# A two-layer Perceiver kernel: the planner that orders its instructions gets measured lengths, overlaps and an exclusion of VectorE and GpSimd, and the context gets one buffer per batch

## The chip, the cores and the metric

The kernel runs on one core of one Trainium2 chip. A core has five engines that each run a queue of instructions in order: PE (TensorE, matrix multiplication), DVE (VectorE), ACT (ScalarE), POOL (GpSimd) and SP (SyncE, which here only issues DMA transfers). The metric is the device time of one execution in microseconds (us); lower is better. The profile is that of one execution on the chip.

## The reference

The input `x` holds 32 batches of 64 tokens by 256 features, `ctx` holds 32 batches of 256 context tokens by 256. Six blocks follow each other, each added to `x`:

```python
x = x + L0_xattn(ctx, layernorm(x))   # q = LN(x) Wq; k, v = [LN(ctx), LN(x)] Wkv; 16 heads of 64; softmax over 320 keys; Wo
x = x + L0_attn(layernorm(x))         # linear attention: relu(q), relu(k), kv = k^T v, q kv / (q sum k), then a layer norm
x = x + L0_ffn(layernorm(x))          # silu(x Wg) * (x Wu) Wd, int8-valued weights, hidden 768
x = x + L1_xattn(layernorm(x), ctx)   # 16 heads of 16, masked softmax over 256 keys
x = x + L1_attn(layernorm(x))         # sLSTM: gated recurrence over 64 tokens, 64 units
x = x + L1_ffn(layernorm(x))          # router with entmax over 8 experts, then each expert's 256-1024-256 MLP
```

All of it is float32. The 2048 tokens make 16 tiles of 128 tokens, two batches each.

## The kernel before, in words

*Stages.* The first cross attention (L0) runs over batches `b` (32), tiles `t` of two batches (16) and groups `g` of four batches (8). `l0_context(t)` loads the context of the two batches of a tile, normalises it (`norm`) and multiplies and adds the layer norm's weights (`affine`, two GpSimd instructions). `l0_queries(g)` makes the queries of a group, then folds the key weights into them (`pqk`, `qk`). `l0_keys(b)` transposes the context (`tr_c`). `l0_scores(b)` makes eight score tiles `sc` of 128 x 320 per batch; for each, VectorE takes the maximum (`nmax`) and ScalarE the exponential; then VectorE scales four of them at once (128 x 1280), and turns them in blocks of 32 x 32 (three `transpose`). The blocks are put into `pT` by sixteen copies of 32 x 640: four on GpSimd, four on ScalarE or VectorE, eight as SyncE transfers. `l0_applied(b)` multiplies them with the context (`pu`), `l0_projected(t)` does the value and output weights (`po`, `pw`). Layer 1 and the rest of layer 0 then run in groups of two tiles: `linear_attention` (tiles `lak`, `lakv`, `lakvs`, `lac`, `laq`, `tr_la`), `feed_forward`, `queries`, `keys_values`, `scores` (`xsc`), `weighted` (`xpTp` transposes, `xpo`), `projected`, `slstm_router` (`slg`, `slp`, `tr_me`). Last come the experts: entmax in two parts A and B (`gT_psA`, `gT_psB`), the lists of tokens, gathers with indirect DMAs, `expert` (`tr_xga`, `mepha`, `mepya` for large buckets of tokens, `tr_xgb`, `mephb`, `mepyb` for small ones), and a scatter of each expert's result that adds to `out`.

*Order.* None of this is run as it is written. The calls on `pl` only record operations, each with its rank (a due time), its engine and what it reads and writes. A few matmuls recorded inside `pl.together(length)` are one operation; `pl.either` and `pl.copy` record an operation that ScalarE or VectorE may run. `Plan.run` then simulates the five engines: again and again it takes, among the operations that could be next, the one with the earliest start by its own model (ties by rank), on the engine where it starts first, and issues it. The instructions stay in this order on each engine. Every recorded instruction is therefore issued from one line, L375 (`issue`) before and L420 after, and the profile must be read by tiles. The model's lengths are in `PlanEngine.length` (L470); an operation may not start before its engine is free and its inputs are done, with `HOP` = 0.06 between engines.

*Buffers.* `bank` takes one of eight PSUM banks. The SBUF tiles named `arena` lie in one large tensor, in areas that `ar.put(phase, tag, size, places...)` lays out; an area's places are used in turn, and a tile can be issued only when its place is free. The context's area `cx` (L652) has two places of 1024 elements, each with one tile of two batches (4 x 256 per partition).

## Time and profile before

| what | value |
|---|---|
| time, median of 3 runs | 1632.85 us (1630.63 to 1634.4) |
| the profiled execution: its time | 1633.02 us |
| its span (first to last instruction) | 1631.3 us |
| mean granted PE clock | 0.991 |
| instructions in the span | 25951 |
| moved by DMA | 95.02 MB, 58 GB/s on average |

The busy share of each engine is the sum of its instructions' durations over the span; matmuls are pipelined, so PE counts as busy while several overlap. The span has three parts of different mix: L0 cross attention up to about 850 us, the groups of layer 0 and 1 from there to about 1400, the experts after it. A row of the stage table is one stretch: its length, each engine's busy time with the instructions that started in it, the granted PE clock (1.00 is full speed), the DMA engines' busy share and GB/s. In a list of waits, a row says which tile's instruction waited for which engine and tile, the total, how often, and the longest.

### The profile page before, as it was taken

What the parts mean: (1) busy time and instruction counts of PE and PEld (TensorE: products, weight loads), DVE (VectorE), ACT (ScalarE), POOL (GpSimd) and SP (SyncE); (2) the same over time, 40 slices, a digit from 0 to 9 for tenths busy, and PEclk for the clock granted to TensorE, in tenths of its full rate; (3) what the DMA queues carried; (4) which work ended last, traced back from release to release, by engine and by line L of the source; (5) the groups of instructions that cost most, each with busy time, mean ns of one, the idle gap of its engine ahead of it and who ended that gap; (6) DMA issues with size and microseconds to landing.
All of it is one profiled execution on the core that took longest, in us unless ns stands there. A gap on an engine that the chain in (4) does not pass through costs nothing. (4 is left out here: it accounts for less than half of the span.)

```text
span 1631.3 us, 25951 instructions
## 1 busy us (share of the span) xinstructions
PE 1579.4 (97%) x9226; PEld 1106.8 (68%) x9226; DVE 1088.2 (67%) x3089; ACT 693.8 (43%) x1813; POOL 422.1 (26%) x524
## 2 busy tenths in 40 slices
PE   8999999999999999999989999999999999999996
PEld 6556656565665656666556777777777776878885
DVE  6657666676766757776755788888888788762230
ACT  4434344353533535334421454454544547432332
POOL 5123123230333223331311221221212112223342
PEclk9999999999999999999999999999999999999998
DMA  6112112121112211122121000010000220455391
GB/s 212 38 30 59 38 31 44 38 59 29 39 30 46 47 34 40 30 71 53 38 54 49 14 27 27 18 37 14 27 27 20 85 80 19 133 144 141 69 307 31
DMA packets 95601, 95.02 MB, mean 58 GB/s; under 512 B 9327, under 2 KB 85936, under 8 KB 95472
## 3 DMA queue, kind: packets, MB, share of 16 engines
q1 hardware_dynamic: 89952, 85.41, 19.2%
q0 software_dynamic: 5520, 7.94, 2.4%
q8 instruction: 74, 1.21, 0.3%
q14 instruction: 55, 0.45, 0.1%
HBM read 63.63 MB, written 7.47 MB: 44 GB/s over the span
## 5 line engine op out<-in xcount | busy, mean ns | idle before, releaser
L375 PE MATMUL pu<-arena 128*128 128x512 f32 (+1 forms) x768 | 301.0, 615 | 3.5 <-ACT arena L375 2.8
L375 PE MATMUL sc<-arena 128*128 128x320 f32 x1024 | 290.5, 436 | 0.0
L375 PEld LDWEIGHTS sc<-arena 128*128 128x128 f32 x1024 | 190.8, 190 | 95.3 <-issue 19.2
L375 ACT ACTIVATE arena<-sc,nmax 128x320 f32<-128x320 f32 x256 | 134.4, 527 | 250.3 <-DVE nmax L375 241.8
L375 PEld LDWEIGHTS pu<-arena 128*128 128x128 f32 (+1 forms) x768 | 113.9, 189 | 175.9 <-issue 159.1
L375 POOL COPY arena<-arena 32x640 f32<-32x640 f32 (+1 forms) x161 | 108.9, 676 | 404.1 <-DVE arena L375 300.4
L375 DVE TENSOR_REDUCE nmax<-sc 128x1 f32<-128x320 f32 x256 | 121.8, 484 | 105.5 <-PE sc L375 104.1
L375 POOL TENSOR_TENSOR arena<-arena 128x1024 f32<-128x1024 f32 (+3 forms) x72 | 118.5, 1646 | 166.6 <-DVE arena L375 109.7
L375 ACT ACTIVATE arena<-arena,xnm 128x256 f32<-128x256 f32 x256 | 127.1, 500 | 52.1 <-DVE xnm L375 51.9
L375 DVE COPY arena<-pu 128x512 f32<-128x512 f32 x62 | 42.7, 689 | 115.4 <-PE pu L375 115.2
L375 DVE CUSTOM_DVE_ANT_0 arena<-xsc,arena 128x256 f32<-128x256 f32 x256 | 101.2, 421 | 17.7 <-ACT arena L375 10.3
L375 DVE TENSOR_TENSOR arena<-arena,sm 128x1280 f32<-128x1280 f32 x64 | 108.1, 1690 | 2.2
L375 DVE STREAM_TRANSPOSE arena<-arena 128x512 f32<-128x512 f32 (+1 forms) x192 | 104.4, 594 | 3.6
L375 ACT COPY arena<-pu 128x512 f32<-128x512 f32 x66 | 38.4, 585 | 128.0 <-PE pu L375 128.0
L375 POOL DMA_INDIRECT out<-arena x25 | 39.6, 1585 | 102.8 <-DVE arena L375 71.2
L375 PE MATMUL pqk<-arena 64*128 64x256 f32 x512 | 63.1, 383 | 1.6 <-ACT arena L375 1.6
L375 PE MATMUL xpTp<-ident,arena 128*128 128x128 f32 x512 | 63.6, 274 | 0.9 <-ACT arena L375 0.9
L375 PE MATMUL xak<-arena 128*128 128x512 f32 x128 | 62.3, 610 | 0.0
L375 PEld LDWEIGHTS xpTp<-ident,arena 128*128 128x128 f32 x512 | 56.9, 141 | 7.2 <-DVE arena L375 2.2
L375 PE MATMUL xav<-arena 128*128 128x256 f32 x256 | 61.5, 384 | 0.0
L375 PEld LDWEIGHTS po<-arena 128*64 128x64 f32 x1024 | 55.5, 137 | 8.8 <-issue 8.3
L375 PE MATMUL mepha<-arena 128*128 128x256 f32 x256 | 60.1, 385 | 1.4 <-ACT arena L375 1.4
(395 smaller groups left out, 2800.9 us busy)
## 6 DMA issues: line engine op xcount, KB each, us to landing
arena<-in_m_w SPq DMA_DIRECT2D x26, 1024.0 KB
arena<-arena SPq DMA_DIRECT2D x256, 80.0 KB
arena<-in_ctx SPq DMA_DIRECT2D x32, 256.0 KB
arena<-in_ctxT SPq DMA_DIRECT2D x16, 512.0 KB
x<-in_x SPq DMA_DIRECT2D x16, 128.0 KB
arena<-in_l0x_wkv SPq DMA_DIRECT2D x2, 1024.0 KB
arena<-arena SPq DMA_DIRECT2D x16, 128.0 KB
out<-x SPq DMA_DIRECT2D x16, 128.0 KB
```

The source lines that it names most:

```text
L375: r = getattr(real, name)(*[get(a) for a in args], **{k: get(a) for k, a in kw.items()})
```

## The change

It has three parts.

1. `Plan.run`'s model. An engine counts as free a little before its operation ends (`OVERLAP`: DVE 0.085, ACT 0.11, POOL 0.05); an operation that needs another's result starts 0.03 after it on the same engine and `HOP` after it on another; a group of matmuls counts 0.985 of its length; and the start of an operation that takes a new place or PSUM bank is not before that place is free (`since`, `when`), which before was only added after the choice. `locks` names VectorE operations (three full-size SBUF operands, or a copy or tensor-scalar operation from SBUF to SBUF of 64 elements or more) and all GpSimd operations but memset as excluding each other: one is not planned to start while the other is held.
2. The lengths in `PlanEngine.length`.
3. The context has one tile of 2 x 256 per batch: `cx` has four places of 512, `affine` is called once per batch with width 2 (128 x 512) in place of once per tile with width 4 (128 x 1024), and `l0_keys` and `l0_applied` index the tile of their batch.

What is computed and the number of matmuls stay as they were. The diff, cut to what the text speaks of:

```diff
@@ -161,6 +162,9 @@
     def room(self, t_, k):
         return len(self.free) > k and (not self.in_order or self.asked[self.next + k] is t_)
 
+    def when(self, k):
+        return sorted(self.free)[k]
+
     def take(self, t_):
         self.free.sort()
         self.next += 1
@@ -186,6 +190,10 @@
             return False
         return all(a.next == len(a.asked) and a.live[j] is None for a, j in self.rivals[i])
 
+    def when(self, k):
+        i = (self.next + k) % len(self.places)
+        return max([self.last[i]] + [a.last[j] for a, j in self.rivals[i]])
+
     def take(self, t_):
         i = self.next % len(self.places)
         self.next += 1
@@ -219,6 +227,7 @@
 
     ENGINES = {"PE": "tensor", "DVE": "vector", "ACT": "scalar", "POOL": "gpsimd", "SP": "sync"}
     HOP = 0.06
+    OVERLAP = {"DVE": 0.085, "ACT": 0.11, "POOL": 0.05}
 
     def __init__(self, tc):
         self.tc, self.ops, self.slots, self.news = tc, [], {}, []
@@ -254,7 +263,7 @@
         self.group = []
         yield
         calls, self.group = self.group, None
-        self.add({"PE": (length, calls)})
+        self.add({"PE": (0.985 * length, calls)})
 
     def add(self, ways):
         op = Op()
@@ -300,6 +309,8 @@
         free = dict.fromkeys(self.ENGINES, 0.0)
         busy = dict.fromkeys(self.ENGINES, 0.0)
         wire = 0.0
+        hold = {"DVE": (0.0, 0.0), "POOL": (0.0, 0.0)}
+        calls_lock = self.locks
         ready = [op for op in self.ops if op.left == 0]
         todo = len(self.ops)
         waiting = set(self.ops)
@@ -318,12 +329,17 @@
                     if "PE" in op.ways and (short is None or op.rank < short.rank) and self.has_room(op, True):
                         short = op
                     continue
+                since = self.since(op)
                 for engine, (length, _) in op.ways.items():
-                    at = free[engine]
+                    at = max(free[engine], since)
                     for other in op.before:
-                        at = max(at, other.end if other.on == engine and other.end == other.done else other.done + self.HOP)
+                        at = max(at, other.done + (0.03 if other.on == engine else self.HOP))
                     for t_ in op.uses:
                         at = max(at, t_.free_at)
+                    if engine in hold:
+                        (lo, hi), other = hold[engine], calls_lock(op.ways[engine][1][0], engine)
+                        if other and lo <= at < hi:
+                            at = hi
                     key = at, op.rank
                     if best is None or key < best[0]:
                         best = key, op, engine
@@ -334,8 +350,11 @@
             ready.remove(op)
             waiting.remove(op)
             op.on = engine
-            op.end = op.done = free[engine] = at + length
+            op.end = op.done = at + length
+            free[engine] = op.end - self.OVERLAP.get(engine, 0.0)
             busy[engine] += length
+            if engine in hold and self.locks(calls[0], engine):
+                hold["POOL" if engine == "DVE" else "DVE"] = at, op.end
             if "dma" in calls[0][0]:
                 size = PlanEngine.size_of(calls[0])
                 wire = max(wire, op.end) + size / 380e3
@@ -347,6 +366,22 @@
                     ready.append(other)
         self.now, self.busy = max(op.done for op in self.ops), busy
 
+    @staticmethod
+    def locks(call, engine):
+
+        name, args, kw = call
+        if engine == "POOL":
+            return name != "memset"
+        if name not in ("tensor_tensor", "scalar_tensor_tensor", "tensor_copy", "tensor_scalar"):
+            return False
+        views = [a for a in list(args) + list(kw.values()) if isinstance(a, View)]
+        size = [math.prod(v.shape[1:]) for v in views]
+        views = [v for v, n in zip(views, size) if n == max(size)]
+        inner = [v for v in views if not isinstance(v.tile.slots, Slots) or v.tile.slots.in_order]
+        if name in ("tensor_tensor", "scalar_tensor_tensor"):
+            return len(inner) >= 3
+        return max(size) >= 64 and len(inner) == len(views)
+
     def has_room(self, op, later=False):
 
         taken = {}
@@ -359,6 +394,16 @@
                 return False
             taken[id(s_)] = k + 1
         return True
+
+    def since(self, op):
+
+        at, taken = 0.0, {}
+        for t_ in op.news:
+            k = taken.get(id(t_.slots), 0)
+            taken[id(t_.slots)] = k + 1
+            if t_ in op.uses:
+                at = max(at, t_.slots.when(k))
+        return at
 
     def issue(self, op, engine, calls):
         for t_ in op.news:
@@ -483,15 +528,17 @@
                 m *= k
             n = max(n, m)
         if name == "memset":
-            return 0.1 + 0.5e-3 * n
+            return 0.12 + 0.5e-3 * n
         if engine == "ACT":
             if isinstance(kw.get("scale"), View):
                 return 0.6
-            return (0.12 + 0.91e-3 * n if name == "copy" else 0.33 + 0.66e-3 * n) + (0.19 if "accum_out" in kw else 0)
+            return (0.12 + 0.91e-3 * n if name == "copy" else min(0.33 + 0.66e-3 * n, 0.6)) + (0.09 if "accum_out" in kw else 0)
         if engine == "DVE":
-            return 0.15 + 1.04e-3 * n + (0.08 if name == "tensor_tensor_reduce" else 0)
+            return 0.15 + 1.04e-3 * n + (0.02 if name == "tensor_tensor_reduce" else 0)
         if engine == "POOL":
-            return 0.7 if n < 64 else 0.3 + 2.0e-3 * n
+            if n < 64:
+                return 0.7 if n <= 2 else 1.0
+            return 0.15 + 0.97e-3 * n if name == "tensor_copy" else 0.3 + 1.9e-3 * n
         return 0.18 if name == "transpose" else max(0.36, 1.67e-3 * n)
 
 
@@ -649,7 +696,7 @@
         ar.put(1, "gb", 1024, 10240)
         for n, tag in enumerate(("la", "ls", "latT")):
             ar.put(1, tag, 512, 11264 + 512 * n, 12800 + 512 * n)
-        ar.put(1, "cx", 1024, 14336, 15360)
+        ar.put(1, "cx", 512, *range(14336, 16384, 512))
         ar.put(1, "cT", 640, 16384, 17024)
         ar.put(0, "gbcol", 256, 17664, 17920)
         ar.put(1, "qk", 1024, *range(17664, 25856, 1024))
@@ -774,12 +821,11 @@
         def l0_context(t):
 
             pl.rank = 2 * t - 6.0
-            cx = ar.tile([P, 4, D], F32, tag="cx", name=f"cx{t}")
+            cx = [ar.tile([P, 2, D], F32, tag="cx", name=f"cx{t}_{b2}") for b2 in range(2)]
             for b2 in range(2):
                 b = 2 * t + b2
                 pl.sync.dma_start(
-                    out=cx[:, 2 * b2 : 2 * b2 + 2, :],
-                    in_=d["ctx"][b * S2 : (b + 1) * S2, :].rearrange("(t p) d -> p t d", p=P),
+                    out=cx[b2], in_=d["ctx"][b * S2 : (b + 1) * S2, :].rearrange("(t p) d -> p t d", p=P)
                 )
             if t == 0:
                 load_w(wv, "l0x_wkv", slice(1024, 2048))
@@ -794,9 +840,10 @@
                 pl.sync.dma_start(out=nxt["rows_a"], in_=d["rows"][:, 0 : 4 * D].to_broadcast([P, 4 * D]))
                 pl.sync.dma_start(out=rows, in_=d["rows"][:, 4 * D :].to_broadcast([P, NROWS - 4 * D]))
             pl.rank = 2 * t - 3.0
-            srcs = [cx[:, i, :] for i in range(4)]
+            srcs = [cx[i // 2][:, i % 2, :] for i in range(4)]
             norm(srcs, srcs, f"c{t}", "c")
-            affine(cx, 0, 4)
+            for b2 in range(2):
+                affine(cx[b2], 0, 2)
             return cx
 
         def l0_queries(g):
@@ -861,7 +908,7 @@
             with pl.together(T4):
                 for kd in range(KD):
                     for i in range(2):
-                        tr(pst[:, kd, i * P : (i + 1) * P], cx[:, 2 * b2 + i, kd * P : (kd + 1) * P], ident)
+                        tr(pst[:, kd, i * P : (i + 1) * P], cx[b2][:, i, kd * P : (kd + 1) * P], ident)
             pl.gpsimd.tensor_copy(cT[:, :, S2:SK], lt[:, :, b4 * S : (b4 + 1) * S])
             pl.copy(cT[:, :, 0:S2], pst)
             return cT
@@ -936,7 +983,7 @@
                     with pl.together(1.75):
                         for n in range(2):
                             rhs = pT[:, 2 * n + jj].rearrange("p a j c -> p j a c")
-                            mm(pus[jj], cx[:, 2 * b2 + n, f_], rhs, start=(n == 0), stop=False)
+                            mm(pus[jj], cx[b2][:, n, f_], rhs, start=(n == 0), stop=False)
                 with pl.together(1.04):
                     for jj in range(2):
                         h_ = slice(64 * jj, 64 * jj + 64)
```

More of the change, by code (lines that the diff above doesn't have):

```diff
@@ L1 @@
+import math
 from contextlib import ExitStack, contextmanager
```

## The prediction

> **What bounds the kernel now.** I read the page's busy shares first, then busy time by stage, then the list of what the TensorE (PE) waits for, then the timeline at the longest waits.
>
> ```profile
> PE 1579.4 (97%) x9226; PEld 1106.8 (68%) x9226; DVE 1088.2 (67%) x3089; ACT 693.8 (43%) x1813; POOL 422.1 (26%) x524
> ```
>
> PE has work for 97% of the 1631.3 us, so the program is a chain of matmuls with holes in it. No other engine is near its limit over the whole. The change touches no matmul, so all that it can gain lies in the holes. Where they are (columns of the stage table: stretch in us, its length, busy time of PE, PE weight load, VectorE, ScalarE, GpSimd with instruction counts, granted clock, DMA share, GB/s):
>
> ```profile
> 0.00:20.00 20.00, 12.22 (x46) 9.70 (x47) 9.72 (x39) 7.18 (x13) 8.54 (x28) 1.00 0.91 302
> ...
> 68.00:95.00 27.00, 23.93 (x99) 13.20 (x96) 20.16 (x39) 10.62 (x28) 7.14 (x10) 0.94 0.31 69
> 95.00:790.00 695.00, 692.80 (x3351) 436.98 (x3352) 473.17 (x919) 294.26 (x715) 196.71 (x194) 1.00 0.19 41
> 790.00:850.00 60.00, 54.28 (x240) 31.82 (x238) 35.80 (x62) 20.95 (x53) 9.12 (x15) 0.98 0.19 43
> ...
> 905.00:1300.00 395.00, 389.66 (x2979) 291.47 (x2980) 318.71 (x1149) 196.69 (x571) 76.02 (x142) 1.00 0.09 29
> 1300.00:1400.00 100.00, 95.76 (x801) 71.66 (x797) 83.66 (x341) 61.74 (x185) 18.33 (x33) 1.00 0.21 67
> ...
> 1568.00:1600.00 32.00, 28.00 (x164) 24.68 (x163) 10.88 (x65) 7.21 (x23) 18.15 (x17) 0.89 0.80 243
> 1600.00:1631.30 31.30, 17.52 (x113) 15.93 (x111) 2.76 (x7) 7.35 (x22) 4.73 (x4) 0.85 0.08 10
> ```
>
> PE's idle time is length less busy. The long cross-attention stretch (95–790) leaves 2.2 us of 695; the start 7.8, the seam of the first two layers 5.7, six layer-1 groups 5.3, the end of layer 1 4.2, the end of the experts 4.0, the last 31 us 13.8 (the last matmul ends at 1617.5; a scatter and the closing follow). In all 52 us. Busy time hides a part: matmul records overlap (a 320-column record is 436 ns long, but they start every 269 ns), so each wait is 0.16–0.19 us longer than its gap. The waits:
>
> ```profile
> PE lakvs L375 <- DVE arena L375: 5.3, 1, 5.3
> PE gbp L375 <- DVE tok L610: 5.3, 1, 5.3
> PE pu L375 <- ACT arena L375: 2.8, 1, 2.8
> PE gT_psB L375 <- DVE arena L375: 2.4, 1, 2.4
> PE xpo L375 <- DVE arena L375: 2.1, 11, 0.2
> PE mephb L375 <- issue: 2.0, 2, 1.2
> PE tr_la L375 <- ACT arena L375: 1.8, 5, 0.4
> PE pqk L375 <- ACT arena L375: 1.6, 7, 0.2
> ```
>
> Five are single places, the rest recur. Some are followed by a half-speed clock:
>
> ```profile
> 79.10:82.50 3.40, 2.88 (x4) 1.37 (x5) 3.24 (x6) 0.06 (x1) 0.00 (x0) 0.50 0.00 0
> 847.10:854.00 6.90, 3.37 (x24) 2.75 (x25) 5.83 (x19) 1.44 (x2) 3.22 (x5) 0.51 0.50 95
> ```
>
> **The change part by part.** I compared both programs' instruction orders. The 9226 matmul records' worth of work is the same. VectorE goes from 3089 to 3053 instructions, ScalarE from 1300 to 1336 (queue counts without accumulator reads), GpSimd from 538 to 570.
>
> *Context in one buffer per batch.* GpSimd runs two 128x512 affine operations where it ran one of 128x1024, 32 times: 2 x 1351 − 2526 ns = +0.18 us each, +5.6 us in all. GpSimd is busy 26–28% there, so its idle time hides it; uncovered it would cost those 5.6. SyncE issues the same 448 instructions; the context loads stay in pairs at the same queue places, and only the two swaps of the latents move behind eight more pT transfers, which is one batch (about 26 us; 27 batches fill 95–790); they stay issued more than two batches ahead of the group that reads them, and that slack hides the move. Zero.
>
> *Exclusion of VectorE and GpSimd.* The row: the softmax scaling, `TENSOR_TENSOR arena<-arena,sm 128x1280`, takes 1690 ns on average (64 times), and 1491–1493 where GpSimd is quiet: 64 x 0.2 = 13 us of blocking. The Trainium skill, "SBUF — State Buffer", section "SBUF: two separate sides", calls the shared port an exclusive lock, where the second instruction blocks fully. Read as time, that rule promises up to 13 us. The row beside it says otherwise: VectorE is 68% busy in 95–790 (473 of 695) while PE lacks 2.2 us, so the 13 us lie beside matmuls. I count nothing for the lock itself, and it speaks against the change that keeping an instruction back delays it for certain to avoid a delay that wasn't on the path.
>
> *Recalibrated lengths and `since`.* These only reorder. By place:
>
> 1. Mode changes of PE. Before, each batch runs 12 `sc`, 12 `pu`, 4 `sc`; after, they interleave, yet changes between full and 64-row matmuls fall from 410 to 399. One costs about 0.2 us (523 against 429 ns at the step into 64 rows, +104 at the way out): **−2**.
> 2. `pu` of batch 1. Its wait is 2.94 us, and half clock for 3.4 us costs 1.7 more. PE's work between its last `sc` and it grows from 9.5 to 11.0 us. The Trainium skill, "TensorE: Matmul & The Clock Gate", section "HAM oscillation", warns of idle gaps over some 3.4 us; this row throttles after 2.9. By the rule the place is worth 1.5; by the row up to 3.2. I go by the row, halfway: **−2.3** (−1.5 to −3.5).
> 3. Steady cross attention. The `pqk` waits (7 x 0.60, for a bank that ScalarE's copy frees; `since` now sees this) and three at `pu` (0.37) total 5.3. Between a batch's last `sc` and its `pu` there are now 15–17 us of PE work (before 12.7–18); the chain needs about 11.3 (point 4). **−4** (0 to −6).
> 4. The seam. From the last `sc` of batch 31 (842.7) the chain is softmax, scaling, transposes to 847.5, eight transfers, `pu` at 854.0: 11.3 us.
>
> ```profile
> 842.70 1.88 PE L375 MATMUL lakv<-arena 128*128 128x512 f32 x4
> ...
> 847.20 5.16 SPq L375 DMA_DIRECT2D arena<-arena  x8
> ...
> 850.54 1.23 PE L375 MATMUL lakvs<-arena 64*128 64x129 f32 x8 [5.32 <-DVE arena L375]
> ...
> 854.03 2.38 PE L375 MATMUL pu<-arena 128*128 128x512 f32 x5
> ```
>
> After, 26 us of work stand between the second `lakv` and its `lakvs`, so that 5.5 us wait goes; but only 3.0 us (before 4.1) stand ahead of this `pu`, which then waits 8 us or more itself. Net: 1.1 us less cover, 0.4 for a VectorE operation now ahead of the transposes, and 0 to 1.7 of half clock: **+2.5** (+1 to +3.5).
> 5. Regular layer-1 groups (67.4 us each). Waits per group: `tr_la` 0.79, `xpo` 0.92, `tr_me` 0.31, `slg` 0.18, so 2.2, and 13 over six groups. Cover grows at `slp`→`tr_me` (4.1 to 5.5) and `xaq`→`xsc` (3.7 to 18.5), stays 0.6 at `xpTp`→`xpo`, and shrinks at `xsc`→`xpTp` of odd tiles (5.5 to 4.3, and 5.8 to 5.2, where about 4.1 is needed), `slg`→`slp` (5.7 to 4.7, 4.15 needed) and `tr_la`→`laq` (3.0 to 1.7). I take half: **−6** (−13 to +5).
> 6. End of layer 1, same joints, 8 us of waits: **−3** (−8 to +3).
> 7. `gT_psB` at 1450.5: 2.5 us and 1.7 of half clock. Its cover grows from 8.2 to 11 us, 10.7 are needed: **−4** (−2 to −4.2).
> 8. The experts' end. A 128x1 VectorE operation waits for a scatter, ahead of the evacuation that frees a bank for the next matmuls:
>
> ```profile
> 1584.63 0.16 DVE L375 TENSOR_TENSOR arena<-arena 128x1 int32<-128x1 f32 x1 [4.53 <-DMA out<-arena]
> 1585.32 0.42 DVE L375 TENSOR_TENSOR arena<-mepyb,arena 128x256 f32<-128x256 f32 x1 [0.53 <-PE mephb L375]
> ```
>
> From `mephb` at 1581.4 to the next `mephb` at 1595.8 are 14.5 us for 8.05 of spacing, so 6.4 are lost. After, both such evacuations stand ahead of the waiting operation, and ten of 44 gate multiplications go to ScalarE. Against it, the first evacuation is behind some 24 small VectorE operations (before 17): +1. **−5** (−2 to −6.4).
> 9. A `tr_xga` directly before its `mepha` at three places (two before): **+0.9**.
> 10. Joints that only the new order makes, which no view of the old one shows. Lower end 0, since nothing can be under no wait; upper about 8 (20 of the usual 0.4 us); nearest rows are the 0.2–0.6 us waits above: **+3**.
>
> Sum: −2 − 2.3 − 4 + 2.5 − 6 − 3 − 4 − 5 + 0.9 + 3 = −19.9. Against the profiled execution's 1633.0 (span 1631.3; 1.7 around it; 0.2 above the median of 1632.85), that gives **1613 us**. The start (7.8) and the closing (13.8) are kept.
>
> **The rivals.**
>
> A, slower: point 5 turns. Its place is layer 1, where VectorE is 81% busy (318.7 of 395). If two evacuation copies (0.59 each on ScalarE) come to stand ahead at each thinned joint, `xpTp` of odd tiles loses 1.0 x 8, `slp` 0.65 x 8, `laq` 0.6 x 16, together 23 us. Without layer 1 my sum stands at −11, so 1622 + 23 = **1645**; it decides from 11 us, half of that. For it: the shrunk covers, and more copies on ScalarE (`xpTp` 68 to 84). Against: ScalarE is half idle there.
>
> B, no real change: waits move to the next joint, as at the seam, and only the mode changes stay: **1631**. For it: 2.2 us idle in 695. Against: `gT_psB` and the tail are single places with room behind them.
>
> C, larger gain: all of 13 and 8 us in layer 1 go and point 10 is nothing: 1613 − 12 − 3 = **1598**. Against: `xpo` keeps its 0.6 cover.
>
> **How the numbers follow.** Chances: forecast 0.60 (own range 1604 to 1625), A 0.16, B 0.12, C 0.12. The measurement tells 0.2% (3.3 us) from no change. A lies above; B is half within it, half below; the rest is below: faster 0.78, same 0.06, slower 0.16. The range from 1599 to 1636 leaves out half of C and most of A.
>
> **What would show it.** Right: no PE wait near 79.6 and none at `gT_psB`; a `pu` wait of 8 us or more at the seam in place of `lakvs`; no VectorE stall of 4 us ahead of a `mepyb` evacuation; `pqk` gone from the list of waits; the 128x1280 scaling near 1.5 us with no gain of its own. Wrong: layer-1 groups longer than 67.4 us, with `xpTp`, `slp` or `laq` in the waits, or new half-clock stretches.

## The result

The changed kernel takes 1637.88 us (median of 18 runs, 1635.36 to 1641.66) where the kernel before takes 1632.56 beside it: ratio 1.0032, 95% interval 1.0022 to 1.0042. It is slower by 0.3%. I had forecast 1613 and given "slower" 0.16; the time lies above my range.

The profiled execution of the changed kernel spans 1637.4 us. Its page, and the busy time by stage (columns as in the table of before):

```profile
PE 1564.8 (96%) x9226; PEld 1099.7 (67%) x9226; DVE 1010.1 (62%) x3053; ACT 716.2 (44%) x1849; POOL 431.7 (26%) x556
```

```profile
0.00:20.00 20.00, 12.40 (x41) 9.68 (x42) 9.87 (x39) 6.59 (x12) 8.89 (x28) 1.00 0.91 303
...
68.00:95.00 27.00, 25.12 (x118) 14.00 (x118) 20.76 (x44) 12.11 (x30) 7.35 (x10) 1.00 0.31 69
95.00:790.00 695.00, 689.14 (x3352) 437.36 (x3348) 430.98 (x907) 306.24 (x728) 204.96 (x222) 1.00 0.19 41
790.00:850.00 60.00, 52.81 (x254) 32.05 (x252) 36.19 (x73) 22.03 (x54) 10.55 (x16) 0.97 0.21 47
...
905.00:1300.00 395.00, 377.58 (x2943) 282.00 (x2943) 298.28 (x1115) 197.14 (x571) 76.32 (x141) 1.00 0.09 29
1300.00:1400.00 100.00, 94.81 (x785) 71.01 (x784) 80.62 (x346) 59.76 (x177) 18.63 (x33) 0.98 0.16 51
...
1568.00:1600.00 32.00, 28.97 (x177) 26.14 (x176) 11.30 (x73) 9.07 (x28) 16.09 (x15) 0.95 0.96 302
1600.00:1637.40 37.40, 22.72 (x152) 20.35 (x150) 3.60 (x10) 8.78 (x25) 9.30 (x8) 0.88 0.13 26
```

VectorE is 78 us less busy than before (ScalarE 22 more), and yet PE is idle for longer: in the layer-1 groups (905–1300) 17.4 us where it was 5.3. Where the time went is best read between matmuls that both orders have, by the start of the first matmul of a tile in both traces (us). The last column is the same difference between a second profile of each kernel (e15 and e16 below, both from one chip):

| from the start, then from mark to mark | before | changed | difference | second pair |
|---|---|---|---|---|
| to `pu` of batch 1 | 79.62 | 80.19 | +0.6 | −0.5 |
| to `pu` of batch 30 (first cross attention) | 751.55 | 749.83 | −1.7 | −1.9 |
| to the first `ffd` of group 1 (the seam) | 101.64 | 103.60 | +2.0 | +0.1 |
| five regular groups | 337.20 | 343.10 | +5.9 | +5.9 |
| to the first `mephb` (end of layer 1, large buckets) | 269.75 | 270.64 | +0.9 | +1.3 |
| to the last `mepyb` (small buckets) | 77.39 | 75.53 | −1.9 | +1.0 |
| all, from the start to the last matmul | 1617.14 | 1622.89 | +5.8 | +5.9 |

The groups, the first cross attention and the end of layer 1 repeat; the start, the seam and the small buckets do not, so two profiles can't tell there what is the change's and what is the execution's.

The regular groups take 68.63 us in place of 67.41. What PE waits for in 905–1300, the longest rows, first before, then changed (total us, times, longest):

```profile
PE xpo L375 <- DVE arena L375: 1.9, 10, 0.2
PE tr_la L375 <- ACT arena L375: 1.8, 5, 0.4
PE xsc L375 <- DVE arena L375: 0.4, 1, 0.4
```

```profile
PE laq L420 <- DVE arena L420: 7.3, 5, 1.5
PE slp L420 <- DVE arena L420: 5.4, 5, 1.1
PE xrT L420 <- DVE r_xa L420: 2.8, 6, 0.5
PE tr_me L420 <- DVE arena L420: 0.8, 5, 0.2
```

The waits of before are all but gone, as forecast. Three others, longer ones, took their place. Per group, counted from start to start of the matmuls (so with the part that overlapping records hide), `laq` waits 1.63, `slp` 1.15, `xrT` 0.64 and a few small ones 0.2: 3.6 us, against 2.4 of before. The difference, 1.2, is the group's whole loss.

`laq` and `slp` wait for VectorE. The row of `xrT` names `r_xa`, which is VectorE's too, but in the code the `xrT` transposes read only what the GpSimd operation `arena<-xsm,arena` wrote, and it ends 0.01 to 0.02 us before `r_xa` in all six places (lines in the last section). That GpSimd operation in its turn starts 0.17 us after VectorE's reciprocal of `xsm`, which is 0.55 us behind the plan (described below), so the lateness comes from VectorE here as well, one step back.

This is how one of the waits looks, in the timeline of the changed kernel (start, duration, engine, instruction, idle time before it and what ended it; ... marks lines left out):

```profile
960.94 0.54 DVE L420 TENSOR_SCALAR arena<-xaq,pp,hm 128x256 f32<-128x256 f32 x1
961.52 0.56 ACT L420 ACTIVATE arena<-xaq,arena,hm 128x256 f32<-128x256 f32 x1 [0.46 <-DVE arena L420]
962.12 0.54 DVE L420 TENSOR_SCALAR arena<-xaq,pp,hm 128x256 f32<-128x256 f32 x1 [0.63 <-ACT arena L420]
...
962.65 0.68 DVE L420 COPY arena<-tr_la 128x512 f32<-128x512 f32 x1
...
963.39 1.35 PE L420 MATMUL laq<-arena 128*128 128x256 f32 x5 [1.47 <-DVE arena L420]
```

The copy of `tr_la` could have run from 960.2, when its transposes were done. It stood in VectorE's queue behind work that came late. I wrote out the start that the planner had given to each operation and set it beside the trace, relative to the matmuls: at 958 us VectorE is already 1.15 us behind its plan; the evacuations of `xaq` (their copies out of PSUM), which VectorE and ScalarE do by turns, waiting for each other, add 1.0 more. The plan has no wait at `laq` at all. The same list shows where the plan's cover came from (cover is the PE work that stands between an operation's producer and the matmul that needs its result): layer-1 matmul groups are planned too long (planned length, which is the number in the code times 0.985, against the median advance in the trace): `xsc` 1.43 against 1.08, `xpo` 0.79 against 0.51, `slg` 1.58 against 0.95, `lac` 0.89 against 0.62, `lakvs` 0.89 against 0.65, `slp` 0.49 against 0.31. With 4, 8, 2, 2, 2 and 2 of them in a group, the planner sees 6.3 us of matmuls per group that don't exist.

### The profile page after: what moved, and what is told of

It reads as the page before. It is cut to its first block, busy times and chain, and to the rows that moved or that the text cites. A ratio compares the mean times of both kernels' runs of the same rounds, so it can differ in the third digit from the quotient of the medians.

```text
span 1637.4 us, 25998 instructions
## 1 busy us (share of the span) xinstructions
PE 1564.8 (96%) x9226; PEld 1099.7 (67%) x9226; DVE 1010.1 (62%) x3053; ACT 716.2 (44%) x1849; POOL 431.7 (26%) x556
## 5 line engine op out<-in xcount | busy, mean ns | idle before, releaser
L420 PE MATMUL pu<-arena 128*128 128x512 f32 (+1 forms) x768 | 305.9, 616 | 6.9 <-DMA arena<-arena 5.3
L420 POOL COPY arena<-arena 32x640 f32<-32x640 f32 (+1 forms) x161 | 117.2, 728 | 430.7 <-DVE arena L420 389.6
L420 POOL TENSOR_TENSOR arena<-arena 128x512 f32<-128x512 f32 (+2 forms) x104 | 120.5, 1180 | 114.5 <-DVE arena L420 84.2
L420 DVE TENSOR_TENSOR arena<-arena,sm 128x1280 f32<-128x1280 f32 x64 | 100.7, 1573 | 1.9
L420 ACT COPY arena<-arena 32x640 f32<-32x640 f32 x115 | 83.1, 723 | 22.7 <-DVE arena L420 21.3
L420 POOL TENSOR_TENSOR arena<-xsm,arena 128x256 f32<-128x256 f32 x32 | 20.6, 643 | 184.5 <-DVE xsm L420 117.2
L420 PE MATMUL po<-arena 128*64 128x128 f32 x1024 | 61.3, 275 | 2.7 <-DVE arena L420 2.4
L420 PE MATMUL pq<-arena 128*128 128x256 f32 x256 | 60.8, 394 | 1.0 <-ACT arena L420 0.7
```

The costliest lines, as they stand in the source:

```text
L420: r = getattr(real, name)(*[get(a) for a in args], **{k: get(a) for k, a in kw.items()})
```

## The experiments

Theory M: the new model makes a few joints too thin, in layer 1 above all. From the list above it became theory P: it shortens the helpers but leaves the matmuls of layer 1 long, so that the cover it counts isn't there. Rivals: C (the context's buffers cost), S (in e2 to e4: only a shift; from e9 on the letter stands for slack), X (waits that no planner length shows). Before was run beside each set; its median was 1628.2 to 1631.9 there, so ratios are what to compare.

| run | ratio to before, 95% interval | regular group, us | batch 1 to 30, us |
|---|---|---|---|
| before, first profile | 1 | 67.41 | 751.55 |
| changed | 1.0032 (1.0022 to 1.0042) | 68.63 | 749.83 |
| e1 context's buffers alone | 1.0056 (1.0042 to 1.0071) | 67.41 | 753.99 |
| e2 new model in the first layer only | 0.9985 (0.9977 to 0.9992) | 67.40 | 749.87 |
| e3 new model in layer 1 only | 1.0144 (1.0128 to 1.0159) | 68.62 | 753.84 |
| e4 new model in the experts only | 1.0067 (1.0054 to 1.0080) | 67.40 | 753.91 |
| e5 true matmul lengths | 0.9903 (0.9887 to 0.9918) | 66.51 | 750.27 |
| e6 evacuations in turn | 1.0053 (1.0038 to 1.0068) | 69.05 | 756.94 |
| e7 no overlap | 0.9881 (0.9864 to 0.9898) | 65.29 | 752.57 |
| e8 as e2, old context | 0.9983 (0.9974 to 0.9992) | 67.40 | 750.16 |
| e9 no overlap, true matmul lengths | 0.9935 (0.9917 to 0.9952) | 66.51 | 753.01 |
| e10 half overlap | 0.9934 (0.9912 to 0.9957) | 68.2 | 749.83 |
| e11 before with true matmul lengths | 1.0084 (1.0063 to 1.0105) | 67.43 | 751.79 |
| e12 no overlap, no exclusion | 0.9889 (0.9871 to 0.9908) | 64.89 | 756.71 |
| e13 overlap in the first layer only | 0.9854 (0.9830 to 0.9878) | 65.29 | 749.83 |
| e14 overlap after the first layer only | 1.0052 (1.0033 to 1.0071) | 68.62 | 753.00 |
| e15 changed, again | 1.0029 (1.0019 to 1.0038) | 68.61 | 749.82 |
| e17 as e13, exclusion in the first layer only | 0.9851 (0.9833 to 0.9868) | 64.89 | 749.83 |
| e18 as e13, old context | 0.9851 (0.9835 to 0.9866) | 65.29 | 750.14 |

### The change's parts and stages apart (e1 to e4)

e1 is the kernel before with the hunks of `l0_context`, `l0_keys`, `l0_applied` and the `cx` area alone. e2 to e4 are the changed kernel, in which each operation carries the model by which it is costed and placed, switched by stage:

```diff
+        op.new = self.new
...
-                since = self.since(op)
+                since = self.since(op) if op.new else 0.0
...
-            free[engine] = op.end - self.OVERLAP.get(engine, 0.0)
+            free[engine] = op.end - (self.OVERLAP.get(engine, 0.0) if op.new else 0.0)
```

and likewise for the exclusion, the lengths, the 0.985 and the rule for dependents; `self.new` is set by stage while the operations are recorded.

> The kernel before with the third part of the change alone (one context buffer per batch, two affine instructions of 128x512 in place of one of 128x1024), planned by the old model. Theory M (thin joints: the new model's order puts too little matmul work between producer and consumer at a few joints of layer 1, laq, slp and xrT, and at the seam of the first two layers; the context's buffers cost nothing): 1632.6 us, within 2 us of before, layer-1 groups at 67.4 us. Rival C (the 5.6 us of added GpSimd time delay the context and the latents, as the new waits tr_lat <- GpSimd hint): 1636 us or more, with tr_lat waits of 0.7 us in each group of the first layer.

Measured: 1636.5 us where before takes 1629.46. Rival C is right here, and my zero for the buffers wrong under the old model. The `tr_lat` waits that C expected in each group are not there (three in all). By the marks, half of the cost is one wait in the start (`pu` of batch 1 starts at 84.18 us, before at 79.62); batches 1 to 30 take 2.4 us more, and the seam 104.4 where the two profiles of before have 101.64 and 102.93:

```profile
PE tr_lat L375 <- POOL arena L375: 4.2, 2, 4.0
```

```profile
41.02 0.29 POOL L375 COPY arena<-arena 128x128 f32<-128x128 f32 x1 [8.86 <-PE sc L375]
41.59 3.73 POOL L375 TENSOR_TENSOR arena<-arena 128x512 f32<-128x512 f32 x2 [0.27 <-ACT arena L375]
```

GpSimd was idle for 8.9 us at the head of its queue, before a 128x128 copy that waits for `sc` matmuls; the affine of the next group's latents stands behind it, and `tr_lat` waits 4 us for that. In the profile of before the same two affines ran at 35.5 us, ahead of that copy, and took as long (3.92 us against 3.73). So at this place the added instructions cost by the order that they brought, not by their length.

> The changed kernel, but only the first cross attention is planned and costed by the new model; layer 1 and the experts by the old one. Theory M: the first layer keeps its gain of about 3 us at batch 28, layer-1 groups go back from 68.7 to 67.4 us, tail as before: 1629 us if the seam is no worse than before, 1633 if the seam's loss of about 5 us belongs to the first layer's new order. Rival C: 1636 or more, since the context's buffers are in. Rival S (the change is no better anywhere, its gains in the first layer are only a shift of where work stands): 1634 to 1637.

Measured: 1626.59 us against 1629.46: faster by 0.15%, groups back at 67.40. With the buffers in, the new model in the first layer gains all that they lose (e1) and more. M is right; C and S fall for this version.

> The changed kernel, but only the layer-0 and layer-1 groups after the first cross attention are planned and costed by the new model; the first cross attention and the experts by the old one. Theory M: the groups take 68.7 us in place of 67.4, six of them and the end of layer 1 cost 8 to 12: 1640 to 1644 us, with laq, slp and xrT at the top of the list of waits and no seam wait for pu of more than before. Rival C: 1636, as in the run with the context's buffers alone. Rival S: 1634 to 1637.

Measured: 1652.71 us, nearly 9 more than M's highest. Groups at 68.62 and `laq`, `slp`, `xrT` on top, as M says. The rest is e1's loss in the first layer, and 279.2 us from the last regular group to the first `mephb` (before: 269.75), where layer-1 work in the new order meets the experts in the old one. That mixture is in neither kernel; only the group's time is read from this run.

> The changed kernel, but only the experts (from the first entmax on) are planned and costed by the new model; both layers before by the old one. Theory M: the stretch from the first mephb to the end gains about 2 us, gT_psB's wait of 2.5 us with its half clock goes and comes back at rlb: 1630 us. Rival C: 1636. Rival S: 1632 to 1634.

Measured: 1639.31 us, where M said 1630: M had not counted e1's loss. Its profile is of an execution at the low end of its runs (1632.55), so I take only one thing from it: against e1 the new model in the experts shows no gain (1.0067 beside 1.0056, with intervals that overlap), though `gT_psB` no longer waits. In its list of waits `rlb` (2.5 us) and `tr_me` (2.0) wait instead, as in the changed kernel (2.24 and 2.51).

### Which lengths (e5 to e7, e9 to e11)

e5: the six numbers in `pl.together(...)` of layer 1 (in the diff, in this order and without the lines between them: `lakvs`, `lac`, `xsc`, `xpo`, `slg`, `slp`).

```diff
-                with pl.together(0.9):
+                with pl.together(0.66):
-                with pl.together(0.9):
+                with pl.together(0.63):
-            with pl.together(1.45):
+            with pl.together(1.10):
-                with pl.together(0.8):
+                with pl.together(0.52):
-                with pl.together(1.6):
+                with pl.together(0.97):
-                with pl.together(0.5):
+                with pl.together(0.32):
```

> The changed kernel, where only six numbers differ: the lengths that the planner gives to matmul groups of layer 1 are set to the spacing in the trace of the changed kernel (xsc 1.45 to 1.10, xpo 0.8 to 0.52, slg 1.6 to 0.97, lakvs 0.9 to 0.66, lac 0.9 to 0.63, slp 0.5 to 0.32). Theory P (the new model shortens the helpers' lengths to about the true ones but leaves these matmuls 0.2 to 0.6 us too long each, some 6 us per group; so it counts cover at the joints that isn't there, and the helpers arrive late at laq, slp and xrT): the three waits shrink from 3.4 us per group to about 1, groups take 66 to 66.5 us in place of 68.7, the whole 12 to 16 us less than the changed kernel. Rival X (the waits come from what the planner can't see: the two engines that evacuate xaq in turn wait for each other, and small VectorE operations are blocked by GpSimd): groups stay at 68.3 to 69, laq still waits 1.6.

Measured: 1612.59 us where before takes 1628.77, some 21 less than the changed kernel (1.0032 times 1628.77 is 1634.0). Groups 66.51. PE's waits in 905–1300, the longest rows:

```profile
PE tr_la L420 <- DVE arena L420: 3.3, 5, 0.7
PE tr_ff L420 <- ACT arena L420: 1.9, 2, 1.7
PE xpo L420 <- DVE arena L420: 1.4, 5, 0.3
```

`laq`, `slp` and `xrT` are gone. P is right in place and sign; it gained more than I expected, since the end of layer 1 gains too (261.1 us to the first `mephb`, 270.6 in the changed kernel).

e6: the planner's test for a dependency takes the whole stretch between first and last element of a view.

```diff
-                    if any(a <= d and c <= b for a, b in runs for c, d in others):
+                    if runs[0][0] <= others[-1][1] and others[0][0] <= runs[-1][1]:
```

> The changed kernel with one line of the planner altered: two writes to one tile whose strided places interleave count as dependent, as the waits in the trace show them to be (the four evacuations of xaq, two on VectorE and two on ScalarE, wait for each other by turns for 0.5 to 0.6 us). Rival X: the wait at laq falls from 1.6 to 0.7 us or less and the groups from 68.7 to 67.8 us. Theory P: the matmuls keep their order, the VectorE copy ahead of laq moves by one or two places, the groups stay within 0.4 us of 68.7.

Measured: 1637.04 us, groups 69.05. PE's waits in 905–1300, the longest rows:

```profile
PE tr_ff L420 <- DVE arena L420: 7.3, 6, 1.4
PE slp L420 <- DVE arena L420: 5.6, 5, 1.3
PE xrT L420 <- DVE r_xa L420: 2.4, 5, 0.5
```

X's first half falls: the wait at `laq` did shrink, to 0.38, but `tr_ff`, the next transposes, then wait 1.58. The edit doesn't take the turns away; it lets the plan count them, and that does not shorten the group. It acts on the whole kernel, and the first layer got longer by it (756.94). X's second half, small VectorE operations blocked by GpSimd, e6 does not test; the last section comes back to it.

e7: the table emptied.

```diff
-    OVERLAP = {"DVE": 0.085, "ACT": 0.11, "POOL": 0.05}
+    OVERLAP = {}
```

> The changed kernel without the table of overlaps (an engine counts as busy to the end of its operation, as before); the rest of the new model stays. VectorE then counts 0.085 us more per instruction, about 12 us more per layer-1 group. Theory P: the helpers' lengths are again too long, as the matmuls' are, the joints get cover and the groups go back to 67.2 to 67.8 us: 4 to 8 us less than the changed kernel. Rival X: the waits at laq and slp do not depend on it, groups at 68.3 to 69.

Measured: 1608.59 us, groups 65.29, two below the lowest that P allowed. What is left of waits in 905–1300:

```profile
PE xsc L420 <- ACT arena L420: 1.8, 5, 0.4
PE ffg L420 <- DVE arena L420: 0.7, 1, 0.7
PE xsc L420 <- DVE arena L420: 0.4, 1, 0.4
```

So the overlap table alone turns a gain of 1.2% into a loss of 0.3%. The overlap itself is real: half of VectorE's instructions in the profile of before, and two thirds in that of the changed kernel, start before the one ahead of them ends, by 82 ns in the median. It harms by what it does to the plan. Whether the plan wants truth (T) or slack (S), the next three were to tell. e9 joins e5 and e7; e10 has half of each overlap; e11 puts e5's numbers into the kernel before.

> The changed kernel without the table of overlaps and with the six matmul lengths of layer 1 set to the trace's spacing: both single changes that brought it to 1608.6 and 1612.6. Theory S (what pays is slack: the planner keeps cover at the joints when it takes the helpers for slower, or the matmuls for faster, than they are): the two add in part, groups at 65.3 us or less, 1600 to 1606 us where before takes 1629. Rival T (what pays is truth: with true matmul lengths the overlaps, which the trace shows to be real, should help, so leaving them out costs): groups at 66.3 us or more, 1611 to 1617.

> The changed kernel with half of each overlap (VectorE 0.0425, ScalarE 0.055, GpSimd 0.025). Theory S: between both ends, groups at 66 to 68 us (65.3 without, 68.7 with the whole), 1615 to 1630 us. Rival U (a list scheduler's order jumps; any small change of a length moves the time by as much, and the overlap is no cause by itself): outside of that, below 1612 or above 1634.

> The kernel before (old model, one context buffer per tile) with the six matmul lengths of layer 1 set to the trace's spacing. Theory S: the old model already takes the helpers for slower than they are, true matmul lengths add cover: groups go from 67.4 to 66.5 us or less, 1617 to 1624 us beside 1629 of before. Rival T: the old model's helpers are too long for true matmuls, no gain: groups at 67.2 us or more, 1626 to 1634.

Measured: e9 1618.6 us and groups 66.51, e10 1619.62 and groups 68.2, e11 1643.21 and groups 67.43 (before beside them 1628.22). e9 speaks against S: more slack was worse than either alone. T has e9's groups right and its time 1.6 us too low. e10's time lies between, as S says, but its runs spread from 1610 to 1622 us and most of its groups are near the changed kernel's, just outside S. e11 fits neither: groups as before, and the loss at the end of layer 1 (284.3 us to the first `mephb`). With true matmul lengths and the long helper lengths of the old model, the plan is worse; with true matmul lengths and short helpers better. That leans to lengths that fit each other, but e7, whose matmuls are long and whose helpers are a little long, has the best groups of the three. Which set of lengths gives the best order I can't say from these runs; that the two single corrections each undo the loss is shown, why both together gain less is open. Nor do they rule out rival U, that any small change of a length moves the order as much: the same six numbers made the changed kernel 1.3% faster and the kernel before 0.8% slower. What is shown is what this table does in this kernel.

### The exclusion and the context (e8, e12, e17, e18)

> As the run with the new first layer, but with the context in one buffer per tile as before (part three undone): only the new model in the first cross attention is left of the change. Theory C2 (the buffers cost time under the new model as well: the tr_lat waits for GpSimd of 0.76 us in five groups, and 1.3 us of the start): tr_lat leaves the list of waits, 3 to 5 us less than with the buffers, 1622 to 1624 us beside 1629.5 of before. Rival D (the new model needs the second place: the context of a tile comes later, new waits at tr_c or sc): as with the buffers or slower, 1627 or more.

Measured: 1626.49 us, with the buffers (e2) 1626.59. C2 falls: the `tr_lat` waits stay (3.4 us in five) without the buffers, so they come from the new model's order on GpSimd. D's new waits at `tr_c` or `sc` are not there either: the buffers change nothing here.

e12 makes `locks` return False, on top of e7.

> The changed kernel without the table of overlaps, and with the exclusion of VectorE and GpSimd left out of the planner as well. As forecast before the result (the blocking lies beside matmuls and is worth nothing on the path): the 128x1280 scaling goes from 1602 ns back to 1660 to 1700, and the time stays within 4 us of 1608.6 where before takes 1629. Rival L (the exclusion earns its keep): 1613 us or more, with waits of PE on VectorE or GpSimd that are not there with it.

Measured: ratio 0.9889 beside e7's 0.9881. As forecast, the exclusion is worth nothing in sum, and L falls. By place it is not nothing: between batches 1 and 30 the first layer loses 4.1 us without it, and the layer-1 groups gain 0.4 each. What I had wrong is the scaling's duration, here in the changed kernel, in e12 and in e1:

```profile
L420 DVE TENSOR_TENSOR arena<-arena,sm 128x1280 f32<-128x1280 f32 x64 | 100.7, 1573 | 1.9
```

```profile
L419 DVE TENSOR_TENSOR arena<-arena,sm 128x1280 f32<-128x1280 f32 x64 | 101.9, 1592 | 1.9
```

```profile
L375 DVE TENSOR_TENSOR arena<-arena,sm 128x1280 f32<-128x1280 f32 x64 | 96.9, 1514 | 2.2
```

It fell from 1690 to 1573 ns, and stays at 1592 without the exclusion (1602 in e7, with it), so the exclusion is not what shortens it. The context's buffers alone, under the old model, bring it to 1514 (e1), the new model without them to 1607 (e8). The time does not follow it: e1 has the shortest scaling of these, 11 us less in all than before, and is slower than before. That fits the forecast that these 13 us lie beside matmuls.

> The changed kernel with both the overlaps and the exclusion of VectorE and GpSimd kept in the first cross attention and left out after it, where the groups took 64.9 us without either (65.3 without overlaps alone). Theory O: the first layer stays at 749.8 us, groups 64.9, the whole 0.981 to 0.985 of before. Rival (the exclusion earns its keep at the end of layer 1): 0.988 or more.

> The run with overlaps in the first layer only, with the context in one buffer per tile as before: part three undone in the fastest version. As in the pair with only the new first layer (1626.6 with the buffers per batch, 1626.5 without), the buffers are worth nothing under the new model: within 0.2% of the ratio 0.9854 to before. Rival C: 0.982 or less, with the tr_lat waits gone.

Measured: e17 1606.4 us and e18 1607.28 where before takes 1630.95, both 0.9851, which is the 0.9854 of e13 (below) within the intervals. In this version neither the context's buffers nor the exclusion after the first layer is to blame or earns anything; the exclusion within the first layer is in all three. e17's groups are at 64.89 and its first layer at 749.83, as expected; with a median of 1606.4 (1.5% faster than before) it is the fastest here together with e18.

### Where the overlap harms, and the experts' end (e13 to e16)

e13 applies the overlap to operations of the first cross attention only, e14 to all others only:

```diff
-            free[engine] = op.end - self.OVERLAP.get(engine, 0.0)
+            free[engine] = op.end - (self.OVERLAP.get(engine, 0.0) if op.ovl else 0.0)
```

> The changed kernel with the overlaps kept in the first cross attention and left out for everything after it. The matmuls then stand in the first layer as in the changed kernel and from there on as in the run without overlaps. Theory O (the overlap's harm sits in layer 1 and the experts alone; in the first layer it gains): groups 65.3 us, first layer (batch 1 to batch 30) 749.8 us as changed where the run without overlaps took 752.6, 1604 to 1609 us where before takes 1629. Rival V (the gain without overlaps comes from the first layer or the seam): 1620 us or more.

> The mirror of it: overlaps left out in the first cross attention, kept for everything after it. Theory O: groups 68.6 us as changed, first layer 752.6, 1634 to 1640 us. Rival V: 1622 us or less.

Measured: e13 1609.64 us, e14 1641.27, where before takes 1631.93. The stages come out as expected: first layer 749.83 with the overlap and 753.00 without (752.6 expected), groups 65.29 without and 68.62 with. The totals are 0.6 and 1.3 us above O's ranges. Theory O holds; V falls. The same table gains 3 us in one stage and loses 3.3 us per group in the other.

> The changed kernel once more, on the chip of these runs, for its profile beside that of the kernel before from the same chip. Theory E (the experts' end differs from execution to execution for the same order of instructions: 77.4 us from the first mephb to the last mepyb in the profile of before, but 72.0, 72.3 and 71.9 in three runs that kept the experts' order; so my term of -5 for that end was read from one execution): 70 to 76 us for this stretch, not the 75.5 of its first profile to the tenth; groups 68.6 as before. Rival (the stretch belongs to the order): 75.5 within 0.5 us.

> The kernel before once more, for one profile. Theory E: 70 to 73 us from the first mephb to the last mepyb where its first profile had 77.4, no 4.5 us wait of VectorE for a scatter ahead of a mepyb evacuation, and groups at 67.4 as before. Rival (the stretch belongs to the order): 77.4 within 0.5 us.

Measured, from the first `mephb` to the last `mepyb` in their profiles: e15 76.23 us, e16 75.23, with e13 75.50 and e14 75.82 on the same chip. Theory E misses both (narrowly for e15, and e16 has a wait of 4.8 us where E expected none), and the rival misses both too. The profiles of all runs have only a few orders of instructions in this stretch, so they can be sorted by order and by chip (e10, e12 and e17 have other orders):

| order of the stretch | first pair | chip 14 | chip 9 | chip 10 |
|---|---|---|---|---|
| of before | 77.39 | e1 71.98, e2 72.27, e3 73.38, e11 71.23 | e8 71.92 | e16 75.23 |
| of the changed kernel | 75.53 | e4 70.34 | e5 70.51, e6 70.23 | e14 75.82, e15 76.23 |
| of e7 | | e9 73.67 | e7 69.54 | e13 75.50, e18 73.98 |

One order differs by 6 us between executions. On one chip the orders differ by less, as far as single executions tell: that of the changed kernel is 0.9 to 3.0 us shorter than that of before on chip 14, 1.4 to 1.7 on chip 9, and 0.6 to 1.0 longer on chip 10. So the larger part of the 6.4 us does not belong to the order of instructions, and what the changed order gives is 3 us at most here. What makes the rest differ is not shown. DMA engines are busy for 96% of 1568–1600 in the changed kernel, and VectorE waits 4 to 5 us there in both kernels. In the profile of before, taken again (e16), for an indirect scatter, and in the changed kernel:

```profile
1585.73 0.18 DVE L375 TENSOR_TENSOR arena<-arena 128x1 int32<-128x1 f32 x1 [4.83 <-DMA out<-arena]
1585.84 0.41 DVE L375 TENSOR_TENSOR arena<-mepyb,arena 128x256 f32<-128x256 f32 x1
```

```profile
1592.26 0.42 DVE L420 TENSOR_TENSOR arena<-mepyb,arena 128x256 f32<-128x256 f32 x1 [4.45 <-remote]
...
1592.74 0.71 PE L420 MATMUL mephb<-arena 128*128 128x128 f32 x4 [2.28 <-issue]
```

The evacuation now does stand ahead of the 128x1 operation, as I had read from the orders. It waits 4.45 us by itself, for something that the profile names only "remote".

## Why the prediction was wrong

*Points 1, 3 and 10, the first layer.* Forecast −2, −4 and, with the joints that only the new order makes, +3. Measured −1.7 from batch 1 to 30. The `pqk` waits did leave the list. In their place, in 95–790, came:

```profile
PE tr_lat L420 <- POOL arena L420: 3.4, 5, 0.7
PE po L420 <- DVE arena L420: 2.4, 6, 0.4
```

`tr_lat` waits for GpSimd (5 x 0.76) and `po` for VectorE (6 x 0.58), 7.3 us where before lost 5.3: point 10 alone needed more here than I gave it for the whole kernel. With 2.0 us more of waits the stage still got 1.7 shorter, so 3.7 us came from elsewhere. Point 1 can be only a part of it: from batch 1 to 30 the traces have 163 changes of the array's form before and 156 after, and those into and out of 64 rows did not fall (130 and 132). Where the rest comes from is not shown, so the near hit of the sum is luck.

*Point 2.* Forecast −2.3. The wait fell from 2.94 to 1.74 us and the half clock after it is gone (granted clock 1.00 in 68–95, before 0.94): from the first `pu` of batch 0 to that of batch 2, 48.85 us became 46.16, −2.7 (49.00 and 46.16 in the second pair). Right. The gain does not show in the table because `pu` of batch 0 starts 1.8 us later in this execution; e2, with the same matmul order in this stage, starts it 3.5 us earlier.

*Point 4, the seam.* Forecast +2.5 (+1 to +3.5), measured +2.0 in the first pair and +0.1 in the second, where before itself took 1.3 us longer. The mechanism was right in part:

```profile
845.93 1.01 PE L420 MATMUL lac<-arena 128*64 128x136 f32 x8 [3.35 <-DVE arena L420]
852.25 6.04 PE L420 MATMUL pu<-arena 128*128 128x512 f32 x8 [5.31 <-DMA arena<-arena]
```

`lakvs` no longer waits, but the wait of 8 us or more came as two, 3.4 at `lac` and 5.3 at `pu`, and half clock lasts for 10.2 us there (846.8 to 857.1) where it lasted 6.8.

*Point 5, the regular groups.* This is the step that failed. Forecast −6 for six groups; measured +1.22 each, +7.3 (five of them, +5.9 in both pairs, in the table above). I had listed the very joints that got thin (`tr_la`→`laq` 3.0 to 1.7, `slg`→`slp` 5.7 to 4.7) and took "half" of the gain all the same. `laq` and `slp` did wait, 1.63 and 1.15; `xpTp`, which I had as the worst, did not, and `xrT`, which I had not listed, waited 0.64. Rival A had the place and two of its three joints, and its sign; its mechanism, evacuation copies ahead on ScalarE, is not what the trace shows: VectorE, 1.15 us behind the plan and then held up by the `xaq` evacuations. My measure was at fault: I compared cover with what a chain takes when its helpers are free (4.15, 4.1), and not with how late VectorE's queue already runs at that place. What makes the order so thin there is shown by taking parts away: without the overlap table the groups take 65.29 us (e7, e13), with true matmul lengths 66.51 (e5). My forecast had put the "recalibrated lengths" down as something that only reorders and never asked whether the lengths still fitted each other.

*Points 6, 7 and 9.* Forecast −3, −4 and +0.9; measured +0.9 together (+1.3 in the second pair). `gT_psB` no longer waits, but `rlb` does, 2.24, and `tr_me`, 2.51, the latter for one wait:

```profile
PE tr_me L420 <- DVE arena L420: 3.2, 6, 2.3
PE rlb L420 <- DVE arena L420: 2.2, 1, 2.2
```

A stall that moved on, which I had refused to believe for a "single place". And the end of layer 1 got a stall that before doesn't have: `tr_ff` waits for ScalarE, and half clock follows, one of the signs that I had named for being wrong:

```profile
1306.37 0.55 PE L420 MATMUL tr_ff<-ident,arena 128*128 128x128 f32 x3 [1.68 <-ACT arena L420]
```

```profile
1307.60:1311.00 3.40, 3.40 (x12) 2.94 (x11) 1.01 (x3) 0.96 (x2) 0.62 (x1) 0.50 0.02 5
```

With 1.7 us for half clock that is 3.4 us, in both profiles of the changed kernel.

*Point 8.* Forecast −5; −1.9 between the first profiles and +1.0 between the two on one chip. The 6.4 us lost there were read from one execution and put down to the order. By the table of e15 and e16 the order gives 3 us at most, and on chip 10 nothing.

*The parts counted at nothing.* The exclusion: right in sum (e12, e17). The context's buffers: right under the new model (e2 and e8, e13 and e18), wrong under the old one (e1, +0.56%), for a reason in GpSimd's queue order and not in the added 0.18 us that I had costed.

Together, by the table: point 5 missed by 12 us (its −6 against +5.9), points 6, 7 and 9 by 7, point 8 by 3, the start with point 2 by 3, the first layer by 1, and the seam gave 0.5 back. That is 25.5, about what lies between 1613 and 1637.9. Only the shares of points 5, 6, 7 and 9 and of the first layer are about the same in both pairs of profiles; in the second, point 8 missed by 6 and the seam gave 2.4 back.

## What to carry to other kernels

To make one kind of work's lengths in a planner truer while another's stay too long can cost more than the error did; truth in all of them was not the best here either. So after each calibration compare planned with measured starts, stage by stage, and keep the table only where it pays (here: the overlaps in the first layer alone, 1.5% faster than before). When a new order is judged from the old trace, cover at a joint must be compared with how late the helper's queue runs there, and a thinner joint counts as a wait until shown otherwise. A loss seen in one execution near DMA-bound work is not the order's until a second execution shows it.

## What the runs showed of the hardware

A VectorE operation of 128 x 2 elements took 0.57 us instead of 0.15 beside a 128x256 GpSimd operation, six times in the changed kernel, once per group; both ended within 0.02 us of each other. Shown with them are the reciprocal, whose result the GpSimd operation reads, and the `xrT` transposes:

```profile
951.76 0.19 DVE L420 RECIPROCAL xsm<-xsm 128x8 f32<-128x8 f32 x1
...
952.12 0.73 POOL L420 TENSOR_TENSOR arena<-xsm,arena 128x256 f32<-128x256 f32 x1 [2.36 <-PE xpTp L420]
952.29 0.57 DVE L420 SCALAR_TENSOR_TENSOR r_xa<-t_xa,r_xa 128x2 f32<-128x2 f32 x1
...
952.90 0.20 PEld L420 LDWEIGHTS xrT<-ident,arena 128*128 128x128 f32 x2 [0.71 <-POOL arena L420]
952.90 0.44 PE L420 MATMUL xrT<-ident,arena 128*128 128x128 f32 x2 [0.48 <-DVE r_xa L420]
```

So the blocking that I had costed on the 128x1280 scaling alone also holds up small operations. It isn't every GpSimd operation that does: in the profile of before, operations of this kind that ran beside the 128x2 GpSimd operations (`r_la`, `r_lay`) took 0.15 to 0.16 us. And it need not cost anything: `xrT` reads the GpSimd result and not `r_xa` (the row of its weight load names GpSimd), and in e11 `r_xa` is held up six times as well, with groups at 67.43.

A wait of 2.5 us was followed by half clock in the profile of before (`gT_psB`), but not in that of the changed kernel (`tr_me`, at 1437.9; granted clock 1.00 in 1400–1450), and there the 1.7 us of `tr_ff` at 1306.4 were followed by it, while the 1.5 us of `laq` were not, in any of five groups. The length of a wait alone does not decide it in this range.
